# Fewer held expert tiles, shorter inverse roots and a moved scale, gate and check in a two-layer transformer kernel

## The chip, the core and the metric

The kernel runs on one core of one Trainium2 chip. The metric is the device time of one execution in microseconds (us). A core has TensorE (PE, matrix products and transposes through the PE), VectorE (DVE), ScalarE (ACT), GpSimd (POOL) and SyncE (SP); the queues of SP and POOL issue nearly all transfers here. Each engine works through its own list of instructions in order, and the engines wait for each other by semaphores.

## What is computed

Four batches of 1024 rows with 256 channels, in fp32, go through two layers. Each layer is an attention and an experts' part, and both add to x. In short:

```python
mod = (silu(c) @ wmod).reshape(4, 6, 1, 256)        # per layer: sa, ca, ga, sb, cb, gb
ga, gb = sign(ga) * max(|ga|, 0.25), sign(gb) * max(|gb|, 0.25)
x = x + ga * attention(layernorm(x) * (1 + ca) + sa)
x = x + gb * experts(layernorm(x) * (1 + cb) + sb)
```

- Layer 0's attention is causal softmax attention over 16 heads with a latent of 64. Its experts' part sends each row to the 2 of 16 experts with the largest router probability: W1, a layer norm of the hidden 256, gelu, W2, and a weighted sum of the two.
- Layer 1's attention is linear (relu, cube, normalised sums) with a convolution of three taps. Its experts' part sends each row to 1 of 8 experts, one matrix and a bias, weighted by the probability.

## The kernel before

**Stages.** `two_layers` runs four stages: the softmax attention (0 to about 510 us), `Experts0.run` (510 to 769), the linear attention (769 to about 996) and `Experts1.run` (996 to the end). x stays on chip in `k.x[b]`. The router and the sort of a batch run inside the stage before the experts that use them.

**Who sets the order.** The program is written in one order, and a planner with a cost model places each engine's instructions by that order and by when it believes the inputs to be ready. `k.pin` fixes an instruction behind the one written just before it on its engine. On top of that `Around` interleaves by hand: `tasks` are generators that yield the weight of each piece (1 or 0.5), and `k.around.step(pieces, rides)` advances the first task by that many pieces and the first of the `riders` by that many rides. Each ride issues one indirect transfer on POOL, which waits for `k.anchor`, the last big matmul written before it.

**Sorted rows.** `Sorting` (L812) counts how many rows each expert has and gives each expert whole tiles of 128 rows. `most_tiles` is the most that any routing can need: 47 tiles for each half of layer 0 (2048 rows, two experts each) and 23, 15 and 15 for the three parts of layer 1 (batches 0 and 1, batch 2, batch 3: `PARTS`). The experts run over all of them, with the expert of a tile read as an offset. `send` (L1111, L1810) fetches rows from `rows_in` and scatters them row by row into `sorted0` or `sorted1` (L928); `combine` (L1346, L1910) gathers the results back (L938) and adds them to x. The sorted buffers are cleared once with zeros on SP (L964).

**First experts.** Groups of four tiles: `arrive` (transposes, copy), `hidden` (W1, bias, statistics), `normalised` (the inverse root, then ACT), `turned` (transposes, gelu), `output` (W2, bias, store). A group's output is written two groups after its hidden part. `second_half` drains all tasks and riders before the other half's rows are loaded: at n + 2 == most, with `most` the number of groups in a half. At the start of the stage batch 3's rows (`Experts0.rows`) and the second half's sort are still tasks. The weights w2 and b2 are loaded behind the first two groups' rows.

**Inverse roots.** `rsqrt` (L72) is a bit-trick seed and three Newton steps, 13 small DVE operations. It is called for each group of the first experts and in `row_statistics` (L94), once per batch for each of the four layer norms.

**Modulation.** `setup_mod` (L166) leaves shift and scale of the attention in transposed form (`k.modT`); the experts' shift, scale and gate are stored and loaded as rows spread over the partitions (`spread_rows`, L202).

**Last experts.** `routed_rows` (L980) normalises on ACT (L992), multiplies by scale and adds shift on DVE (L1006, L1007) and stores the result in `rows_in` (L1009). `tiles_of` takes two tiles: transposes (L1870), an ACT copy (L1872), products (L1877), bias (L1883), store (L1884). `combine` weighs a gathered row on ACT (L1929), multiplies by the gate (L1937) and adds to x (L1938) on DVE in pairs, then stores the output (L1940).

**The check.** Sums that were divided by are kept, and `count_within` (L482) counts with four DVE operations over 128x512 how many lie in bounds: one count in `second_half`, two at the end of the linear attention. `out_of_bounds` (L491) adds them after the first part of the last experts; if any is out, a general version of everything runs (`tc.If(again > 0)`).

## Time and profile before

| | us |
|---|---|
| median of 3 runs (lowest, highest) | 1128.66 (1125.79, 1131.34) |
| the profiled execution | 1116.6 |
| its span, first to last instruction | 1114.8 |
| PE busy, share of the span | 966.1 (87%) |
| DVE busy | 647.1 (58%) |
| ACT busy | 612.0 (55%) |
| POOL busy | 337.5 (30%) |
| mean granted PE clock | 0.952 |
| chain that ended last | PE 63%, DVE 18%, ACT 6%, issue 5%, DMA 5% |

A timeline line gives start, length, engine, source line, operation, tiles written and read, and in brackets the idle time before it with what ended it. A matmul of fp32 counts as two instructions, so a group of four tiles has sixteen for W1 and sixteen for W2, and eight transposes. A DMA issued on SP or POOL stands as an instruction of SPq or POOL; its transfer goes on after that.

### The profile page before, as it was taken

What the parts mean: (1) busy time and instruction counts of PE and PEld (TensorE: products, weight loads), DVE (VectorE), ACT (ScalarE), POOL (GpSimd) and SP (SyncE); (2) the same over time, 40 slices, a digit from 0 to 9 for tenths busy, and PEclk for the clock granted to TensorE, in tenths of its full rate; (3) what the DMA queues carried; (4) which work ended last, traced back from release to release, by engine and by line L of the source; (5) the groups of instructions that cost most, each with busy time, mean ns of one, the idle gap of its engine ahead of it and who ended that gap; (6) DMA issues with size and microseconds to landing.
All of it is one profiled execution on the core that took longest, in us unless ns stands there. A gap on an engine that the chain in (4) does not pass through costs nothing.

```text
span 1114.8 us, 18591 instructions
## 1 busy us (share of the span) xinstructions
PE 966.1 (87%) x6158; PEld 578.1 (52%) x6158; DVE 647.1 (58%) x2143; ACT 612.0 (55%) x986; POOL 337.5 (30%) x528
## 2 busy tenths in 40 slices
PE   4999999999999998986889998887996989758761
PEld 2533434343444343335678887775564656547650
DVE  5924227313562446218767788882899969675452
ACT  0378655756476556872646765655644755423331
POOL 2022222212132156660046125301550100642732
PEclk9999999999999999998999999898998999889986
DMA  6994000000010012826446546414223201457873
GB/s 198 332 347 143 1 1 25 20 1 1 5 58 1 1 57 81 318 97 253 133 152 211 173 147 198 122 55 143 61 67 140 83 20 29 145 170 231 271 228 111
DMA packets 99016, 134.62 MB, mean 121 GB/s; under 512 B 8744, under 2 KB 86088, under 8 KB 98400
## 3 DMA queue, kind: packets, MB, share of 16 engines
q1 hardware_dynamic: 86528, 98.97, 26.6%
q0 software_dynamic: 11776, 33.57, 9.7%
q8 instruction: 53, 0.87, 0.3%
q10 hardware_dynamic: 608, 0.79, 0.2%
q14 instruction: 51, 0.42, 0.1%
HBM read 69.55 MB, written 63.75 MB: 120 GB/s over the span
## 4 chain that ended last, share of the span: by engine, by line
PE 63%; DVE 18%; ACT 6%; issue 5%; DMA 5%; POOL 1%; DVEq 0%; SPq 0%; POOLq 0%; ACTq 0%
PE ps_s L378 12%; PE ps_av L443 11%; PE ps_y L1266 6%; PE ps_qk L354 5%; PE ps_k L1456 4%; PE ps_h L1200 3%; PE ps_v L339 3%; PE ps_out L417 3%; PE ps_pr L1554 3%; DMA ys<-results,index 3%; PE ps_y L1877 2%; PE ps_q L1482 2%; PE ps_lnT L1018 1%; DVE ln_st L101 1%; ACT hid L1224 1%
## 5 line engine op out<-in xcount | busy, mean ns | idle before, releaser
L386 ACT ACTIVATE pT<-ps_s 128x1024 f32<-128x1024 f32 x288 | 279.3, 1021 | 164.3 <-PE ps_s L378 162.3
L389 POOL TENSOR_SCALAR_AFFINE_SELECT pT<-pT 128x256 f32<-128x256 f32 x256 | 105.7, 438 | 324.0 <-ACT pT L386 319.3
L378 PE MATMUL ps_s<-qT,kT 32*128 32x512 f32 (+3 forms) x1536 | 178.5, 520 | 0.5 <-ACT pT L386 0.5
L443 PE MATMUL ps_av<-pT,v 128*32 128x512 f32 (+3 forms) x1536 | 164.2, 495 | 9.7 <-DVE turned L401 6.4
L938 POOL DMA_INDIRECT ys<-results,index x96 | 101.3, 1055 | 136.7 <-DVE mv L1212 35.5
L928 POOL DMA_INDIRECT sorted<-hs,index x96 | 97.7, 1018 | 143.3 <-PE ps_y L1266 69.3
L378 PEld LDWEIGHTS ps_s<-qT,kT 32*128 32x128 f32 x1536 | 74.4, 183 | 95.5 <-issue 72.9
L1266 PE MATMUL ps_y<-w,act 128*128 x376 | 94.0, 406 | 20.5 <-ACT act L1249 20.5
L1224 ACT ACTIVATE hid<-hid,nmr,rstd 128x256 f32<-128x256 f32 x94 | 49.0, 595 | 85.2 <-DVE nmr L1220 85.1
L443 PEld LDWEIGHTS ps_av<-pT,v 128*32 128x32 f32 x1536 | 40.6, 108 | 102.6 <-issue 56.7
L1266 PEld LDWEIGHTS ps_y<-w,act 128*128 128x128 f32 x376 | 74.8, 205 | 33.8 <-ACT act L1249 23.1
L1200 PE MATMUL ps_h<-w,xT 128*128 x376 | 86.0, 380 | 1.7 <-ACT xT L1183 1.5
L401 DVE STREAM_TRANSPOSE turned<-ps_av 128x512 f32<-128x512 f32 x32 | 22.8, 713 | 97.1 <-PE ps_av L443 96.8
L1200 PEld LDWEIGHTS ps_h<-w,xT 128*128 128x128 f32 x376 | 69.4, 190 | 11.1 <-ACT xT L1183 2.4
L1877 PE MATMUL ps_y<-we,xT 128*128 x212 | 57.1, 416 | 18.5 <-ACT xT L1872 18.0
L1249 ACT ACTIVATE act<-ps_hT,gain 128x128 f32<-128x128 f32 x188 | 67.7, 461 | 4.5 <-PE ps_hT L1240 4.5
L1456 PE MATMUL ps_k<-wqkv,hT 128*128 128x512 f32 x128 | 62.4, 605 | 3.9 <-DMA wqkv<-in_wqkv_dram 3.0
L361 DVE COPY qT<-ps_qk 128x512 f32<-128x512 f32 x16 | 11.1, 691 | 79.1 <-PE ps_qk L354 79.0
L1877 PEld LDWEIGHTS ps_y<-we,xT 128*128 128x128 f32 x212 | 41.5, 207 | 27.6 <-ACT xT L1872 21.5
L1275 DVE TENSOR_TENSOR y<-ps_y,b 128x256 f32<-128x256 f32 x94 | 37.7, 419 | 24.1 <-PE ps_y L1266 23.4
L101 DVE BATCH_NORM_STATS2 ln_st<-x 128x6 f32<-128x256 f32 x128 | 49.2, 409 | 0.5
L1208 DVE TENSOR_TENSOR hid<-ps_h,b 128x256 f32<-128x256 f32 x94 | 36.5, 415 | 20.0 <-PE ps_h L1200 16.4
(218 smaller groups left out, 1526.3 us busy)
## 6 DMA issues: line engine op xcount, KB each, us to landing
xs<-sorted SPq DMA_DIRECT2D x71, 256.0 KB, 4.1
results<-y SPq DMA_DIRECT2D x71, 256.0 KB, 2.4
sorted<-zero SPq DMA_DIRECT2D x2, 6016.0 KB, 21.1
rows_in<-h SPq DMA_DIRECT2D x16, 512.0 KB, 2.9
hs<-rows_in POOLq DMA_DIRECT2D x32, 256.0 KB, 4.0
w<-in_w_dram SPq DMA_DIRECT2D x8, 1024.0 KB, 7.9
x<-in_x_dram SPq DMA_DIRECT2D x4, 1024.0 KB, 8.0
b<-in_b_dram SPq DMA_DIRECT2D x2, 2048.0 KB
```

Of the source, the lines that this page charges most:

```text
L101: nc.vector.bn_stats(st[:, t, :], k.x[b][:, t, :])
L378: k.anchor = nc.tensor.matmul(pair[hh // 2][:, hh % 2, c0 : c0 + w], lhsT=kTs[o][rows, kb * P : (kb + 1) * P], rhs=qT[rows, q1 - w : q1], ...
L386: nc.scalar.activation(pT, ps, AF.Exp, scale=1.0 / L**0.5)
L389: nc.gpsimd.affine_select(out=pT[:, :, c0 : c0 + P], in_=pT[:, :, c0 : c0 + P], compare_op=ALU.is_ge, fill=0.0, base=0, pattern=[[0, 2], [ ...
L443: nc.tensor.matmul(po[32 * hh : 32 * hh + 32, 512 - w :], lhsT=vs[b % 2][:, kb, 8 * g + 2 * hh + o, :], rhs=exps[b, g, o, u][hh // 2][:, h ...
L928: i = self.k.nc.gpsimd.indirect_dma_start(out=buffer.ap, out_offset=bass.IndirectOffsetOnAxis(ap=index, axis=0), in_=rows, in_offset=None, ...
L938: self.paced(self.k.nc.gpsimd.indirect_dma_start(out=rows, out_offset=None, in_=buffer.ap, in_offset=bass.IndirectOffsetOnAxis(ap=index, a ...
L1200: mm = nc.tensor.matmul(ph[:, j], lhsT=xTs[i // 2][:, j, cc], rhs=w1[:, cc, bass.ds(at[i + j], C)], start=cc == 0, stop=cc == CC - 1,)
L1249: o = nc.scalar.activation(act[:, j, cc], pt[:, j, cc], AF.Gelu, bias=gain[:, 1, cc, t : t + 1], scale=gain[:, 0, cc, t : t + 1],)
L1266: mm = nc.tensor.matmul(po[:, j], lhsT=acts[i // 2][:, j, cc], rhs=w2[:, cc, bass.ds(at[i + j], C)], start=cc == 0, stop=cc == CC - 1,)
L1456: k.anchor = nc.tensor.matmul(ps, lhsT=hT[:, cc, t * P : (t + 1) * P], rhs=wqkv[:, cc, C:], start=cc == 0, stop=cc == CC - 1,).ins
L1877: k.anchor = nc.tensor.matmul(po[:, j], lhsT=xT[:, j, cc], rhs=self.we[:, cc, bass.ds(at[j], C)], start=cc == 0, stop=cc == CC - 1,).ins
```

## The change

- **Fewer held tiles.** `held_tiles` holds rows // 128 + 3/4 of the experts: 44 per half, and 22, 14 and 14. One DVE operation per sort (five in all, `k.fits`) notes whether the rows fit; if not, the general version runs. The buffers keep their old size, and the part of the results that is no longer written is cleared with zeros at the same place as the sorted rows (five transfers more).
- **Shorter roots.** 10 operations: another seed, one cubic step and one Newton step.
- **Last batches.** For the parts of one batch (2 and 3) `routed_rows` no longer applies scale and shift. They are applied on ACT with per-partition operands (`k.modF`) at the two copies behind transposes: the router's `hT`, and `xT` in `tiles_of`. The gate is applied to the experts' result before its store, and `combine` becomes one DVE operation a row. The first part is unchanged.
- **Checks later.** All three counts are made in the last experts after the second part, in three row buffers (tag `xs`), and the sum and test after the third part.
- **First groups.** Three pieces of tasks are issued before the weights' loads; group 1 issues none; groups 0 and 1 no longer issue four at their end; in group 2 `turned` follows `hidden`.

The diff, cut:

```diff
-RSQRT_SEED = float(0x5F3759DF - (1 << 31))
+RSQRT_SEED = float(0x5F3759DF - (1 << 22) - (1 << 31))
+CUBIC = 1.5**0.5
...
-    nc.vector.tensor_scalar(half, var, eps, None, ALU.add)
+    nc.vector.tensor_scalar(half, var, eps, 0.5, ALU.add, ALU.mult)
...
-    nc.vector.tensor_scalar(half, half, 0.5, None, ALU.mult)
-    for step in range(3):
-        nc.vector.tensor_tensor(a, src, src, ALU.mult)
-        nc.vector.tensor_tensor(a, a, half, ALU.mult)
-        dst = out if step == 2 else y
-        nc.vector.scalar_tensor_tensor(dst, a, -1.5, src, ALU.add, ALU.mult)
-        src = y
+    nc.vector.tensor_tensor(a, src, src, ALU.mult)
+    nc.vector.scalar_tensor_tensor(a, a, CUBIC, half, ALU.mult, ALU.mult)
+    nc.vector.scalar_tensor_tensor(a, a, -5.0 / 3.0 * CUBIC, a, ALU.add, ALU.mult)
+    nc.vector.scalar_tensor_tensor(y, a, 1.25 * CUBIC * CUBIC, src, ALU.add, ALU.mult)
+    nc.vector.tensor_tensor(a, y, y, ALU.mult)
+    nc.vector.tensor_tensor(a, a, half, ALU.mult)
+    nc.vector.scalar_tensor_tensor(out, a, -1.5, y, ALU.add, ALU.mult)
...
+    for m, (shift, scale) in ((k.modT[layer], ((0, 0), (0, C))), (k.modF, ((32, C), (64, 0)))):
+        if m is k.modF and layer == 0:
+            continue
+        for i, (p, c) in enumerate((shift, scale)):
...
+            nc.vector.tensor_scalar(
+                m[:, CC * i : CC * i + CC], pt[:, :, :B], float(i), None, ALU.add
+            )
...
+def count_sums(k, pool):
+    recs = [k.recs.rearrange("p n i j -> p (n i j)")]
+    recs += [k.recs1[:, i].rearrange("p b t h -> p (b t h)") for i in range(2)]
+    inverse = 1.0 / SUM_HI, 1.0 / SUM_LO
+    for i, (rec, (low, high)) in enumerate(zip(recs, (inverse, (SUM_LO, SUM_HI), inverse))):
+        good = pool.tile([P, 8 * B * H], F32, tag="xs", name="good", bufs=6)
+        count_within(k, good, rec, low, high, k.good[:, i : i + 1])
...
+def held_tiles(k, rows, ne):
+    return most_tiles(rows, ne) if k.fits is None else rows // P + 3 * ne // 4
...
+        if k.fits:
+            nc.vector.tensor_scalar(
+                k.fits.pop(0), ends[:, 1, ne - 1 : ne], float(self.tiles), None, ALU.is_le
+            )
...
+        if scalar and scale is not None:
             nc.vector.tensor_tensor(h, h, bcast(scale, 1, 4), ALU.mult)
             nc.vector.tensor_tensor(h, h, bcast(shift, 1, 4), ALU.add)
...
-            nc.scalar.copy(hT[:, cc], ps)
+            if scale is None:
+                nc.scalar.activation(
+                    hT[:, cc], ps, AF.Identity,
+                    bias=k.modF[:, cc, b : b + 1], scale=k.modF[:, 2 + cc, b : b + 1],
+                )
+            else:
+                nc.scalar.copy(hT[:, cc], ps)
...
-            if early:
-                good = self.back.tile([P, 4, C], F32, tag="out", name="good")
-                count_within(
...
+        if early:
+            k.around.step(3)
         load_weights(w1, b1, "1")
...
-            if last:
+            if last and n > 2:
                 acts = turned(*last)
             now = hidden(hf, tiles, xTs)
-            k.around.step()
+            if last and n == 2:
+                acts = turned(*last)
+            if n != 1:
+                k.around.step()
...
-            k.around.step(2 if last else 4)
+            if last:
+                k.around.step(2)
...
-            nc.scalar.copy(xT[:, :n], ps[:, :n])
+            b = PARTS[p][0] if len(PARTS[p]) == 1 else None
+            if b is None:
+                nc.scalar.copy(xT[:, :n], ps[:, :n])
+            else:
+                for cc in range(CC):
+                    nc.scalar.activation(
+                        xT[:, :n, cc], ps[:, :n, cc], AF.Identity,
+                        bias=k.modF[:, cc, b : b + 1], scale=k.modF[:, 2 + cc, b : b + 1],
+                    )
...
+            if b is not None:
+                nc.vector.tensor_tensor(y[:, :n], y[:, :n], bcast(self.gate[:, b], 1, n), ALU.mult)
...
-                if early and p == 0:
+                if early and p + 2 == len(PARTS):
+                    count_sums(k, work)
+                if early and p + 1 == len(PARTS):
                     again = out_of_bounds(k, work, ps_x)
                 k.around.tasks.append(self.combine(p))
...
-            k.pin(nc.scalar.activation(
-                y[:, j], coming.pop(0), AF.Identity, scale=part[:, n : n + 1]
-            ))
+            if len(PARTS[p]) == 1:
+                xs = k.x[b][:, t]
+                k.pin(nc.vector.scalar_tensor_tensor(
+                    xs, ys, part[:, n : n + 1], xs, ALU.mult, ALU.add
+                ))
...
+        for buffer in k.results0:
+            buffer.clear(zero, held_tiles(k, HT * P * 2, E0))
+        for buffer, p in zip(k.results1, PARTS):
+            buffer.clear(zero, held_tiles(k, len(p) * N, E1))
```

## The prediction on record

> **What bounds the kernel now.** I read the busy slices first, then the busy time by stretch, then each engine's timeline and the waits where a stretch is not full. The slices (27.9 us each) show TensorE nearly full except at the ends of stages, and VectorE (DVE) at 8 or 9 tenths through the middle:
>
> ```profile
> PE   4999999999999998986889998887996989758761
> ...
> DVE  5924227313562446218767788882899969675452
> ```
>
> The stretches (us; its length; busy us of PE, weight loads, DVE, ACT, POOL; granted clock; DMA) are the first experts' stage in four parts, a stretch of the second attention, its end, and the last two of the last experts' stage:
>
> ```profile
> 511.00:595.00 84.00, 65.70 (x365) 54.33 (x364) 61.64 (x276) 46.57 (x100) 17.96 (x19) 0.92 0.58 199
> 595.00:631.00 36.00, 36.00 (x199) 32.12 (x198) 28.37 (x124) 21.47 (x53) 17.25 (x19) 1.00 0.61 201
> ...
> 670.00:770.00 100.00, 83.88 (x418) 71.83 (x416) 76.45 (x337) 59.39 (x146) 26.06 (x37) 0.93 0.38 115
> ...
> 820.00:870.00 50.00, 37.73 (x176) 25.43 (x174) 48.92 (x158) 25.58 (x50) 8.63 (x13) 0.90 0.33 113
> ...
> 960.00:987.00 27.00, 12.51 (x92) 9.92 (x92) 22.42 (x66) 10.29 (x18) 15.21 (x15) 0.76 0.66 212
> ...
> 1068.00:1090.00 22.00, 15.38 (x60) 12.11 (x58) 9.57 (x21) 6.34 (x13) 8.41 (x8) 0.77 0.63 203
> 1090.00:1115.00 25.00, 0.00 (x0) 0.00 (x0) 5.78 (x9) 4.06 (x8) 8.01 (x8) 0.57 0.34 104
> ```
>
> Only 595 to 670 is TensorE's alone. Before it PE idles 18.3 of 84 us, after it 16.1 of 100; 820 to 870 and 960 to 987 are DVE's; from 1090 no matmul runs. The waits of 635 to 770 (total, times, longest) say why PE idles late in the first experts: it waits for activations, and those for the inverse root:
>
> ```profile
> ACT hid L1224 <- DVE nmr L1220: 44.8, 10, 8.0
> ...
> PE ps_y L1266 <- ACT act L1249: 14.9, 6, 4.6
> ```
>
> The rows of the second half come by scatter on POOL, here first, a fetch, and last of 32, then the load that waits for them on SP, then PE at its first use (631.52, no idle noted) and at a later gap:
>
> ```profile
> 562.61 1.01 POOL L928 DMA_INDIRECT sorted<-hs,index  x1 [59.77 <-PE ps_y L1266]
> ...
> 571.05 0.76 POOL L1118 DMA_DIRECT2D hs<-rows_in  x1 [3.59 <-DMA sorted<-hs,index]
> ...
> 621.34 0.97 POOL L928 DMA_INDIRECT sorted<-hs,index  x1 [0.30 <-issue]
> ```
> ```profile
> 626.13 1.90 SPq L971 DMA_DIRECT2D xs<-sorted  x4
> ```
> ```profile
> 628.93 2.76 PE L1200 MATMUL ps_h<-w,xT 128*128 x12
> 631.52 1.04 PE L1177 MATMUL ps_xT<-ident,xs 128*128 128x128 f32 x8
> ...
> 697.90 5.12 PE L1266 MATMUL ps_y<-w,act 128*128 x16 [4.58 <-ACT act L1249]
> ```
>
> The loads were issued 3.8 us after the last scatter and take up to 4.3, so the rows land near 630.4: the scatter has about 1 us to spare. In the last stage a copy that PE needs is queued on ACT behind a gathered row:
>
> ```profile
> 1082.51 0.51 ACT L1929 ACTIVATE out<-ys,part 128x256 f32<-128x256 f32 x1 [1.25 <-DMA ys<-results,index]
> 1082.92 1.05 ACT L1872 COPY xT<-ps_xT 128x512 f32<-128x512 f32 x2
> ```
>
> **What the Trainium skill says.** "VectorE: DVE Perf Modes", section on the TRN2 errata, gives (N+151)/0.96 ns for an fp32 tensor_tensor: 161 ns at N=4, 691 at 512. The trace has 156 (L88, 128x4) and 691 (L1937): a root is bought by the number of its operations. "DMA: Bandwidth & Descriptors", section "Anatomy of one DMA", puts some 2 us of fixed cost on a transfer, most of it the receipt of the last write; here the 3.8 us above. "TensorE: Matmul & The Clock Gate", section "HAM oscillation", says that gaps above 3.4 us drop the clock; after the gap of 4.58 the sixteen matmuls took 5.12 instead of 3.62, so a long gap costs 1.5 more.
>
> **The change, part by part.** The profiled execution took 1116.6 us (span 1114.8), 1.1% under the 1128.66 median; I carry the difference in us over.
>
> *Startup and first attention.* The first root lies on the chain (L81 to L90, 15.72 to 18.15): 3 operations fewer at 0.20 apart, -0.6. Layer 1's modulation gets two more copies (0.17) and four more transposes (about 0.1) at 47 to 49: +0.4. The five added clears (9 tiles of 128 KB, 1.2 MB) go on SP behind 18.8 MB of clears; what is queued behind is the gate of batch 0, issued at 83 and first used at 168. Hidden; uncovered, 1.2 MB at 332 GB/s is 3.5. Sum **-0.2** (-1 to +3).
>
> *First experts, first half.* 47 held tiles become 44. A steady group of four takes 8.66 (602.30 to 610.96), 2.165 a tile, so three are 6.5 of PE. But the second half then starts at group 11 and needs its rows earlier, and the new order delays them. I counted the pieces: batch 3's rows and its sort have 19 or 20 left. Before, groups 0 and 1 issue 5 each and later ones 5; the sort hands over its scatters in group 3, the 32 rides (5 a group) run out in group 9, and group 10's drain finds nothing. After, 3 pieces come first, then 1, 0, 5, 5, 5: hand-over in group 4, and the drain, now in group 9, issues the last 10 scatters together, anchored to that group's hidden matmuls, whose end I call T. Early on, batch 3's normalisation goes ahead of the groups' work, but its store (L1009) then stands on SP before the fetch of group 2, which lands at 529.5 anyway (15.4 us, behind 6 MB of second weights). So T is between 595 (steady from 531) and 615 (as now); I take 605. The last scatter ends no earlier than T + 10 x 1.29 + a fetch 1.1 = 619; and no earlier than its start (565, from 560 to 572) + 32 x 1.29 + 8.4 of fetch waits = 615. Then 3.8 and 4.3: rows at 627, against 631.5 now, and PE, which wanted them at T + 8.7 = 614, has a new gap of 13 us; the clock adds 1.5. **-2.5** (-14 to +10). What is late next is the scatter.
>
> *Second half.* Three tiles, -6.5. Six gaps of y behind an inverse root (697.9 to 765.4), each root 0.6 shorter: -3.6. Dropping the count (4 DVE operations, 2.2 us) in the drain falls where DVE has room: 0. **-10.1** (-14 to -3).
>
> *Second attention.* Two roots in the full stretch 820 to 870: -1.2. At its end two counts leave DVE (0.36+0.42+0.68+0.69 and 0.43+0.43+0.68+0.66 = 4.35) and batch 2's scale and shift (4 x 1.22 = 4.9), of which the chain of waits holds 4.6 between 960 and 987; the rest hides behind the y chain (L1546). The modulated copies on ACT take 0.59 to 0.78 (L1021, L160), four of them: 0, up to +0.8. **-5.8** (-10 to -2).
>
> *Last experts.* Three tiles at 2.16 a pair are 3.2. The first part's is -1.1. The second's buys nothing: that phase (1034 to 1062) is paced by 16 gathers 1.31 apart, begun at 1038.6 and still weighted on ACT. In the third (1062 to 1090) ACT no longer holds the transposed copies behind gathers: gaps 4.5 and 1.9, with slow matmuls after them, go. DVE takes their place: three counts 6.6, seven pairs of bias and gate (0.76+0.69) 10.2, eight weighted adds (0.475, as L1371) 3.8, one bound of 20.6, against 28 now. I add 1.4 for waits: -6. The counts take three of six row buffers; the third waits for pair 18's transposes, and pair 22's load on SP for pair 19's, with results queued behind it: 0 to 2, inside that 1.4. In the tail the last gather was followed by ACT 0.51, gate 0.69, add 0.69 (with hops 2.0); now one operation 0.48: -1.5, and the last pair's gate before its store +0.7. The final test (DVE, PE, DVE, a register load on every engine) sits on POOL ahead of the last eight gathers; it ends about 1.5 us after the last y while the results need 3.3 (1090.28 to 1093.58): 0, to +1.7 if POOL's load (0.51 and 1.23 of issue at 1098) is exposed. **-8** (-13 to +2). Batch 3's missing scale and shift (4.9) shorten a sort whose rows have 20 us to spare: 0.
>
> Sum: -0.2-2.5-10.1-5.8-8 = **-26.6**, 1090.0 on the profiled execution, **1102** on the median.
>
> **Rivals.**
> *The scatter keeps up* (groups compressed fully and a sort near 555): the first half gives -13.5, in all -37.6, 1091. For it: PE's 18.3 idle us before 595. Against: the ten rides in one burst.
> *DVE gives it back*: with 40 us of DVE in the last two phases instead of 25, and a planner that places counts and weighted adds ahead of y, the last stage gives +1 and the second attention half, -2.9; -0.2-2.5-10.1-2.9+1 = -14.7, 1114.
> *Slower: the late sort.* Its pieces now compete in groups 2 to 5 with those groups' own DVE work. If its first scatter, now at 562.6, starts at S, rows come at S+59.7+8.1. The other parts give 24.1, so with 1.5 of clock it decides from S = 562.6+24.1-1.5 = 585. At the early spacing (13 us, from group 2 at 534.5), a sort ending in group 6 gives S = 590 to 594: +5 to +9, 1136. Against: half of its work stands where DVE waited.
> *Nothing gained because the fallback runs*: it would double the time. From the reference's inputs the sorts need 41, 41, 20, 12 and 13 tiles; 44, 44, 22, 14 and 14 are held. Under 1 in 100, inside the slower chance.
>
> **How the numbers follow.** A run set of this kernel can tell about 0.5% (5.6 us) from no change, 1123 to 1134.3. Forecast 0.50 (own range 1094 to 1110), scatter keeps up 0.17, DVE 0.22 (a fifth of it past 1123), late sort 0.11 (just over half of it past 1134.3). Faster: 0.50+0.17+0.18 = 0.85; same 0.04+0.05 = 0.09; slower 0.06. The range 1086 to 1122 leaves out the late sort (0.11), the DVE case past it (0.04) and what lies below 1086 (0.04).
>
> **What would show it.** PE: a gap of 9 to 17 us before the first transposes of group 11, ended by xs loads; POOL: ten scatters 1.3 apart before it. Second half 10 us shorter from there. In 960 to 987 DVE busy falls by 9. In the third phase no gap behind L1929 and DVE near full; the tail some 24 us. I am wrong if the gap before group 11 is absent, if the sort ends after group 5, or if the third phase is not shorter.

## The result, and the profile after

The kernel after takes **1117.56 us** (median of 5 runs, 1114.98 to 1119.15), the kernel before in the same set 1130.0 (1125.79 to 1131.58). The ratio is 0.9892, with an interval of 0.9866 to 0.9918: 12.4 us, where 26.6 had been forecast. Two more sets of the unchanged kernel after gave 0.9858 (0.9820 to 0.9895) and 0.9907 (0.9880 to 0.9933). The gain is about 13 us, 10 to 16 in the three sets.

The profiled execution of the kernel after took 1117.6 us (span 1115.8), its median. The one of the kernel before, from which the forecast was made, had taken 1116.6, 13 us under the 1130.0: the two profiles differ by 1 us, and the gain can't be seen between them. So I profiled the kernel before again (first experiment: 1128.3, span 1126.5) and compare with that one. The stages are cut at the first transposes of sorted rows, the first transposes of the second half, the first of the second attention, and the first of batch 3's projections behind the sort of batch 2:

| profile | start | first half | second half | second attention | last experts | span |
|---|---|---|---|---|---|---|
| before, first profile | 510.1 | 121.4 | 138.0 | 217.6 | 127.7 | 1114.8 |
| before, again | 511.5 | 120.3 | 138.7 | 221.1 | 134.9 | 1126.5 |
| after | 512.5 | 132.1 | 133.1 | 210.1 | 128.0 | 1115.8 |
| after, mean of three profiles | 512.9 | 132.8 | 130.3 | 210.8 | 127.8 | 1114.7 |
| after with the old order, mean of two | 513.1 | 116.7 | 134.1 | 210.8 | 127.9 | 1102.7 |

The old order of the last row is explained with the experiments. In the mean of the three profiles against the second row, one stage got longer, the first half of the first experts, by 12.5; the stages behind it got shorter by 25.8, and the first experts began 1.4 later. The lines that answer to those of before, busy time first, then the slices of PE and DVE (27.9 us each), where the 23rd of PE (614 to 642) shows a hole that was not there:

```profile
PE 952.5 (85%) x6072; PEld 563.6 (51%) x6072; DVE 623.2 (56%) x1987; ACT 602.6 (54%) x959; POOL 336.2 (30%) x528
...
PE   4899999999999998997789589887898798959670
...
DVE  5823236313463455216596556794689978663472
```

The stretches, with the same columns as in the prediction:

```profile
512.50:604.00 91.50, 71.60 (x393) 59.53 (x391) 64.51 (x264) 47.23 (x100) 12.74 (x14) 0.93 0.50 174
604.00:630.00 26.00, 25.47 (x137) 22.29 (x136) 18.79 (x80) 19.10 (x47) 14.86 (x16) 1.00 0.57 177
630.00:660.00 30.00, 15.38 (x80) 13.74 (x81) 11.27 (x48) 9.48 (x23) 7.83 (x9) 0.77 0.48 153
645.00:778.00 133.00, 117.21 (x594) 101.17 (x592) 94.21 (x387) 78.11 (x189) 35.88 (x45) 0.94 0.41 125
828.00:878.00 50.00, 38.42 (x177) 25.68 (x175) 48.99 (x150) 26.38 (x51) 9.11 (x13) 0.90 0.33 115
960.00:987.80 27.80, 16.16 (x120) 11.01 (x118) 18.59 (x65) 15.43 (x26) 17.91 (x19) 0.90 0.48 158
1062.00:1090.00 28.00, 20.09 (x85) 16.32 (x83) 23.07 (x50) 8.90 (x19) 10.88 (x10) 0.84 0.65 206
1092.00:1116.00 24.00, 0.00 (x0) 0.00 (x0) 4.16 (x10) 0.00 (x0) 8.00 (x8) 0.56 0.40 121
```

From 604 to 630 PE is full, and from 630 to 660 it is half idle at a clock of 0.77. The end of the second attention (960 to 987.8) still has DVE at 18.6, and in the third phase of the last experts (1062 to 1090) DVE has 23.1 of 28. The waits of the second half (645 to 778: total, times, longest):

```profile
ACT hid L1269 <- DVE nmr L1265: 27.3, 7, 6.6
...
PE ps_y L1311 <- ACT act L1294: 13.7, 7, 4.3
```

The rows' way in the kernel after: the first scatter on POOL, the first of the last eleven and the last; the loads on SP; then on PE the end of group 9's hidden part and the first use of the second half's rows:

```profile
580.50 1.22 POOL L964 DMA_INDIRECT sorted<-hs,index  x1 [75.27 <-DVE offset L950]
...
626.45 1.01 POOL L964 DMA_INDIRECT sorted<-hs,index  x1 [0.30 <-PE ps_hT L1285]
...
639.28 0.98 POOL L964 DMA_INDIRECT sorted<-hs,index  x1 [0.30 <-issue]
```

```profile
641.85 5.10 SPq L1008 DMA_DIRECT2D xs<-sorted  x6
```

```profile
617.71 3.62 PE L1245 MATMUL ps_h<-w,xT 128*128 x16
...
644.62 1.94 PE L1222 MATMUL ps_xT<-ident,xs 128*128 128x128 f32 x8 [14.63 <-DMA xs<-sorted]
```

The first scatter comes at 580.5, 17.9 later than in the first profile. From 626.45 on the last eleven stand 1.28 apart behind each other with no wait between them, and the loads are issued 2.6 after the start of the last. PE waits 14.63, and its transposes then take 1.94 instead of 1.04. In the last experts two gaps remain. The one in the second phase, behind a gathered row's weighting on ACT (the first part's), was expected to stay; the one in the third, which was to lose its gaps, is a wait for rows whose loads stood behind the counts' row buffers:

```profile
1050.31 3.76 PE L1928 MATMUL ps_y<-we,xT 128*128 x8 [4.35 <-ACT out L1992]
...
1081.57 1.94 PE L1913 MATMUL ps_xT<-ident,xs 128*128 128x128 f32 x8 [5.46 <-DMA xs<-sorted]
```

### The profile page after: what moved, and what is told of

Read it like the earlier page. It is cut to its first block, busy times and chain, and to the rows that moved or that the text cites. A ratio compares the mean times of both kernels' runs of the same rounds, so it can differ in the third digit from the quotient of the medians.

```text
span 1115.8 us, 18093 instructions
## 1 busy us (share of the span) xinstructions
PE 952.5 (85%) x6072; PEld 563.6 (51%) x6072; DVE 623.2 (56%) x1987; ACT 602.6 (54%) x959; POOL 336.2 (30%) x528
## 5 line engine op out<-in xcount | busy, mean ns | idle before, releaser
L1311 PE MATMUL ps_y<-w,act 128*128 x352 | 87.8, 405 | 16.6 <-ACT act L1294 16.0
L1311 PEld LDWEIGHTS ps_y<-w,act 128*128 128x128 f32 x352 | 69.8, 204 | 29.3 <-ACT act L1294 18.3
L1269 ACT ACTIVATE hid<-hid,nmr,rstd 128x256 f32<-128x256 f32 x88 | 45.9, 593 | 67.1 <-DVE nmr L1265 50.8
L1294 ACT ACTIVATE act<-ps_hT,gain 128x128 f32<-128x128 f32 x176 | 63.3, 458 | 15.5 <-PE ps_hT L1285 15.0
L1928 PE MATMUL ps_y<-we,xT 128*128 x200 | 54.3, 418 | 13.3 <-issue 6.0
L1320 DVE TENSOR_TENSOR y<-ps_y,b 128x256 f32<-128x256 f32 x88 | 35.2, 419 | 37.3 <-PE ps_y L1311 21.8
L1928 PEld LDWEIGHTS ps_y<-we,xT 128*128 128x128 f32 x200 | 38.7, 206 | 22.8 <-issue 8.7
L1253 DVE TENSOR_TENSOR hid<-ps_h,b 128x256 f32<-128x256 f32 x88 | 34.2, 416 | 28.6 <-PE ps_h L1245 22.5
```

What stands on the lines that cost most here:

```text
L1269: o = nc.scalar.activation(h[:, i], h[:, i], AF.Identity, bias=nmr[:, i : i + 1], scale=rstd[:, i : i + 1])
L1294: o = nc.scalar.activation(act[:, j, cc], pt[:, j, cc], AF.Gelu, bias=gain[:, 1, cc, t : t + 1], scale=gain[:, 0, cc, t : t + 1],)
L1311: mm = nc.tensor.matmul(po[:, j], lhsT=acts[i // 2][:, j, cc], rhs=w2[:, cc, bass.ds(at[i + j], C)], start=cc == 0, stop=cc == CC - 1,)
L1928: k.anchor = nc.tensor.matmul(po[:, j], lhsT=xT[:, j, cc], rhs=self.we[:, cc, bass.ds(at[j], C)], start=cc == 0, stop=cc == CC - 1,).ins
```

## The experiments

Times are medians; a ratio is always to the kernel before in the same set of runs. Where a kernel is compared in us with one of another set, the kernel before took 1130.0 to 1131.9 in both, unless it is said otherwise.

**The kernel before, unchanged.**

> The kernel before, unchanged. Its profiled execution took 1116.6 us while its runs have a median of 1128.66 to 1130.0. Theory: the profiled execution was an untypical one, so this profile shows a span near 1128, with the missing 12 us at a place that the change touches (the first use of the second half's rows, in the old profile at 631.5, now 5 to 12 later). Rival: the loss is spread over the stages, 2 to 4 us in each, by a granted clock 0.01 lower, and has nothing to do with the change. Second rival: the profile again takes 1116 to 1118 us, and profiling itself makes this kernel faster.

1130.35 against 1131.85, a ratio of 0.9979 (0.9961 to 0.9997) of one kernel to itself: so a difference of 2 us can't be relied on here, whatever its interval. The profile has a span of 1126.5. Neither the theory nor a rival describes it: of the 11.7 that it is longer than the first profile, 7.2 are in the last experts and 3.5 in the second attention, none at the rows' first use (631.78) and none by the mean clock (0.951 against 0.952). The waits of PE that nothing in the profile explains ("issue": total, times, longest) were these in the first profile,

```profile
PE ps_y L1877 <- issue: 0.3, 1, 0.3
...
PE ps_h L1200 <- issue: 0.2, 1, 0.2
```

and these in the new one:

```profile
PE ps_y L1877 <- issue: 4.4, 3, 2.1
...
PE ps_y L1266 <- issue: 2.8, 1, 2.8
...
PE ps_logits L778 <- issue: 2.3, 1, 2.3
...
PE ps_h L1200 <- issue: 0.2, 1, 0.2
```

They come to 0.5 and 9.7 us. All profiles of this study fall in two kinds. In the set where the kernel before takes 1120.4 (the runs from early_pieces to old_counts below), and in the first profile, these waits are 0.0 to 0.5 us on PE; in the sets where it takes 1130 to 1132 they are 2.5 to 17.6. What they are the profile doesn't show; the packets of the main DMA queue took the same time in both (26.6% of 1114.8 and 26.3% of 1126.5 us). The set of 1120.4 ran on one chip, the experiments' other sets on three others; one set can't show that the chip is the reason. The forecast was made on a profile of the first kind and the change measured in sets of the second.

**The order of the first groups alone**, undone in the kernel after and put into the kernel before:

```diff
-        if early:
-            k.around.step(3)
...
-            if last and n > 2:
+            if last:
                 acts = turned(*last)
             now = hidden(hf, tiles, xTs)
-            if last and n == 2:
-                acts = turned(*last)
-            if n != 1:
-                k.around.step()
+            k.around.step()
...
-            if last:
-                k.around.step(2)
+            k.around.step(2 if last else 4)
```

> The kernel after with the old order of the first groups (no three pieces ahead of the weights, a step in every group, the hidden state's transposes ahead of the next group's matmuls throughout). Theory: the new order is what delays batch 3's sort (first scatter 580.5 instead of 562.6); here the first scatter is back at 562 to 568, the gap ahead of group 11's transposes falls from 14.6 to 0 to 6, and the time falls by 8 to 12 against the kernel after, to 1106 to 1110. Rival one: the one group less before the drain makes the gap, the burst of scatters ends no earlier, and the time changes by under 3. Rival two: the new order fills early idle time of TensorE and this kernel is slower than the one after by 2 to 6.

In old_order the new order is undone: 1105.8, ratio 0.9760 (0.9728 to 0.9792), 11.8 under the kernel after, as the theory said. Its scatters are back at the old times, and PE's gap is 4.43:

```profile
564.86 1.01 POOL L964 DMA_INDIRECT sorted<-hs,index  x1 [60.43 <-DVE st L1256]
...
621.20 0.97 POOL L964 DMA_INDIRECT sorted<-hs,index  x1 [0.30 <-issue]
```

```profile
613.18 3.62 PE L1245 MATMUL ps_h<-w,xT 128*128 x16
...
629.89 1.94 PE L1222 MATMUL ps_xT<-ident,xs 128*128 128x128 f32 x8 [4.43 <-DMA xs<-sorted]
```

> The kernel before with the new order of the first groups alone (its 47 tiles, its roots, its counts). Theory: the new order delays batch 3's sort by itself: the first scatter comes at 578 to 584 instead of 564, the second half's rows some 67 later at 645 to 650 instead of 631, and the time rises by 11 to 17, to 1141 to 1147. Rival: here the drain stands one group later, so that the longer first half covers part of it, and the time rises by under 5. Second rival: the order itself gains in groups 0 to 2 and the time falls.

1148.34, ratio 1.0148 (1.0116 to 1.0180): 16.6 slower with nothing changed but the order, the theory again. The time and the first scatter lie a little beyond their ranges, and the rows' first use at 658.5 lies well beyond 645 to 650. The late first scatter, and PE's gap at the end of the half, are here too:

```profile
585.68 1.23 POOL L928 DMA_INDIRECT sorted<-hs,index  x1 [78.62 <-DVE offset L914]
...
647.10 0.97 POOL L928 DMA_INDIRECT sorted<-hs,index  x1 [0.31 <-issue]
```

```profile
658.53 1.94 PE L1177 MATMUL ps_xT<-ident,xs 128*128 128x128 f32 x8 [10.20 <-DMA xs<-sorted]
```

The pair was run once more, side by side:

> The kernel after, unchanged, beside the old order. The executions so far fall in two kinds: where the kernel before takes 1120, TensorE has under 1 us of idle time that nothing in the profile explains; where it takes 1131, it has 5 to 17. Theory: the kernel after gains about the same on both: a ratio of 0.985 to 0.990 if the kernel before is at 1131 here, 0.990 to 0.996 (1109 to 1116) if it is at 1120. Rival: the ratio is the same on both.

> The kernel after with the old order of the first groups, beside the kernel after. Theory: 10 to 15 below the kernel after whichever kind of chip this is. Rival: the new order's cost depends on the chip as the version with the early pieces did (15 to 20 below on one, 2.5 below on another): under 6 here.

1120.85 and 1105.22 (ratios 0.9907 and 0.9761, the latter 0.9726 to 0.9796): 15.6 apart, a little beyond the theory's 10 to 15. The kernel before took 1131.2 here, so the kernel after in a set of the other kind stays unmeasured.

**Which part of the order.** The same kernel with the three pieces ahead and the late transposes of group 2 kept, but the withheld pieces given back:

```diff
-            if n != 1:
-                k.around.step()
+            k.around.step()
...
-            if last:
-                k.around.step(2)
+            k.around.step(2 if last else 4)
```

> The kernel after with its three pieces ahead of the weights and its late transposes in group 2 kept, but with a step in group 1 and the four pieces at the end of groups 0 and 1 given back. Theory: withholding those pieces (1 and 0 instead of 5 and 5) is the whole delay of the sort; here its first scatter comes at 556 to 566 instead of 580.5 and the time is that of the old order or up to 3 below it, 1102 to 1107. Rival: the three pieces ahead put batch 3's normalisation on ScalarE in front of the first rows' copies, and that delays everything: first scatter 568 to 576, 1108 to 1116.

1097.95, ratio 0.9798 (0.9775 to 0.9820), in the set where the kernel before took 1120.4, beside two kernels that both have the new order, no_fold at 1112.0 and old_counts at 1115.9 (below). Its first half took 116.0, theirs 133.5 and 133.4. Their first scatters came at 581.3 and 580.6; that of this kernel:

```profile
560.24 1.01 POOL L964 DMA_INDIRECT sorted<-hs,index  x1 [55.58 <-DVE index L933]
```

So it is the withheld pieces that delay the sort, not those put ahead. How that goes is seen on PE, in batch 3's transposes (ps_lnT), in the ranks that start the sort (ps_rank), and in the last product before it hands over its scatters (ps_gain). The kernel after:

```profile
519.25 6.47 PE L1245 MATMUL ps_h<-w,xT 128*128 x16 [5.71 <-ACT xT L1228]
525.55 0.60 PE L1057 MATMUL ps_lnT<-ident,h 128*128 128x128 f32 x4
...
543.97 0.60 PE L1057 MATMUL ps_lnT<-ident,h 128*128 128x128 f32 x4
...
553.85 0.60 PE L1057 MATMUL ps_lnT<-ident,h 128*128 128x128 f32 x4
...
571.09 0.67 PE L895 MATMUL ps_rank<-some,before 128*128 128x256 f32 x2 [3.22 <-DVE some L890]
...
580.83 0.64 PE L1136 MATMUL ps_gain<-mine,g 16*128 16x44 f32 x4
```

The kernel after with the old order:

```profile
529.56 1.94 PE L1057 MATMUL ps_lnT<-ident,h 128*128 128x128 f32 x8 [7.96 <-DVE h L1046]
...
537.01 1.90 PE L1057 MATMUL ps_lnT<-ident,h 128*128 128x128 f32 x8
...
553.93 0.67 PE L895 MATMUL ps_rank<-some,before 128*128 128x256 f32 x2 [1.47 <-DVE mv L1257]
...
564.51 0.64 PE L1136 MATMUL ps_gain<-mine,g 16*128 16x44 f32 x4
```

The first transposes come 4 us earlier with the new order, but the second set of four is a piece that group 1 no longer issues; it stands behind group 2's hidden part at 543.97, and the last ones come at 553.85 instead of 537.01. The rank comes at 571.1 instead of 553.9, and the hand-over falls into group 5's hidden part instead of group 4's. The 7.96 that PE idles at 529.56 in the old order, waiting for batch 3, are cheaper than that.

**The inverse root alone**, undone in the kernel after (the 13 operations of before) and put into the kernel before:

> The kernel after with the inverse root of 13 operations again. Theory (my terms): 0.6 at the start, 3.6 in six gaps of the first experts' second half, 1.2 in the second attention: 4 to 6 slower. Rival: the gaps are set by ScalarE and the order of the pieces, the operations fall into idle time: slower by under 2. Second rival: a longer root delays the pieces of batch 3's sort too, the first scatter comes 2 to 4 later and the time rises by 7 to 10.

The 13 operations put back into the kernel after (old_roots): 1135.47, ratio 1.0026 (1.0012 to 1.0040), 17.9 slower than the kernel after, more than the theory and its rivals allowed. By the five stages of the table, against the first profile of the kernel after: +4.3, +4.9, +1.6, +4.6, +1.4. The busy time of its page:

```profile
PE 964.5 (85%) x6072; PEld 571.5 (50%) x6072; DVE 635.6 (56%) x2101; ACT 602.8 (53%) x959; POOL 337.0 (30%) x528
```

The same 6072 matmuls took 964.5 instead of 952.5, at a clock of 0.932 instead of 0.945.

> The kernel before with the shorter inverse root alone. Undoing it in the kernel after cost 17.9 us where the sum of its terms had said 5.4. Theory: a root's half microsecond makes gaps that put TensorE's clock down, which is worth as much again or more, wherever it stands: here too it gains 12 to 18, to 1113 to 1119. Rival: the 17.9 are of the kernel after alone (its sort stands on the critical path through the late scatters, and a longer root delays it): here it gains 4 to 7, to 1124 to 1127.

1119.39, ratio 0.9896 (0.9872 to 0.9919): 12.4 faster. The gain is as large as the theory said, but not by its reason: PE's busy time is 969.2 against 967.5 in before_again, so the clock gives nothing here. The stages give +0.5, -1.4, -1.6, -4.0 and -2.2, in sum -8.7 between the two profiles. DVE has 120 instructions fewer (2023 against 2143), which are 40 roots; at 0.6 each (three operations 0.20 apart, as in the prediction) that is an estimate of 24 us, of which 12 show. Why undoing the root costs 17.9 in the one kernel and bringing it gains 12.4 in the other is open.

**Fewer tiles**, two given back to each half of the first experts:

```diff
-    return most_tiles(rows, ne) if k.fits is None else rows // P + 3 * ne // 4
+    return most_tiles(rows, ne) if k.fits is None else rows // P + 3 * ne // 4 + (2 if ne == E0 else 0)
```

> The kernel after with 46 held tiles for the first experts instead of 44 (12 groups a half again instead of 11). Theory: in the first half TensorE waits for the late rows in any case, so two tiles more (4.3 us) fit into the gap of 14.6; in the second half they are paid: slower by 3 to 5, to 1120 to 1123. Rival: both halves pay and a group more brings its own waits: slower by 8 to 10. Second rival: the shorter gap keeps the clock up and the time stays within 2.

1128.51, ratio 0.9976 (0.9959 to 0.9993): 11 slower than the kernel after. That is the first rival, a little beyond its 8 to 10; the theory, that the gap hides the first half's two tiles, fails. The first half is 7.1 longer than the mean of the kernel after, and PE's gap is as long as in the kernel after (14.04): the drain comes a group later too. The last experts were 6.5 longer in this profile, though nothing was changed there, and it lies 6.7 over its own median; how the 11 divide stays open.

**Denser scatters, with the counts in a buffer of their own**, on the old order, and the buffer alone on the kernel after:

```diff
-                k.around.step(rides=1 + i // 2)
+                k.around.step(rides=2 + i // 2)
...
-        good = pool.tile([P, 8 * B * H], F32, tag="xs", name="good", bufs=6)
+        good = pool.tile([P, 8 * B * H], F32, tag="counted", name="good", bufs=1)
```

> The kernel after with the three counts in a buffer of their own instead of three of the six row buffers. Theory: the gap of 5.46 before the third part's transposes at 1081.6 (rows whose load was issued at 1077.1) goes, and the time falls by 3 to 5. Rival: VectorE is full in 1067 to 1084 and only that sets the end, so the gap becomes a wait for VectorE and the time falls by under 1.

With the buffer alone (own_counts) 1115.3, ratio 0.9847 (0.9817 to 0.9878), which can't be told from the three ratios of the kernel after, so that neither the 3 to 5 of the theory nor the rival is shown. In its profile no wait for rows over 1 us is left in the last experts, and that stage takes 125.9 instead of 127.8.

> The kernel after with the old order of the first groups, the counts in a buffer of their own, and two or three scatters a step of the outputs instead of one or two. The old order alone gave 1105.8 and the counts' buffer 2.3 less than the kernel after, 1103.5 together. Theory: the 32 scatters are then limited by the 1.3 each that they take, not by their pacing; they end at 611 to 616 instead of 621.2, the gap of 4.43 ahead of group 11 goes and the clock stays up: 1096 to 1100. Rival: the fetches between the scatters or the sort set the last one: under 2 less, 1101 to 1105. Second rival: denser scatters delay the loads and stores of the running groups: above 1105.

With both on the old order (dense_rides) 1102.88, ratio 0.9758 (0.9731 to 0.9784): the first rival, not the theory. The last scatter comes at 614.1, 7 earlier, and no wait for rows is left ahead of group 11, but the second half begins at 631.0 all the same. PE now waits elsewhere in these groups, for activations, once with a slow group after it:

```profile
601.48 5.41 PE L1311 MATMUL ps_y<-w,act 128*128 x16 [1.78 <-ACT act L1294]
...
623.07 3.72 PE L1311 MATMUL ps_y<-w,act 128*128 x16 [1.64 <-ACT act L1294]
```

> The same as early_pieces, with the counts in a buffer of their own and two or three scatters a step of the outputs instead of one or two. Theory: with an earlier sort and denser scatters the rows are there before TensorE asks for them, and the start of the second half is TensorE's own: 1097 to 1102. Rival: the rows were not late in the dense version either (1102.9), the groups' activations are what ends the waits: 1101 to 1105. Second rival: it is worse than both, over 1106, if the pieces ahead of the weights hurt.

1095.09, ratio 0.9780 (0.9756 to 0.9804), in the set of 1120.4: the lowest time of the study, 2.9 under early_pieces beside it, and PE waits for no rows in its first half. In a set of the other kind:

> The kernel after, unchanged, beside the other three of this call, since the chips differ (the kernel before took 1131.8 on one and 1120.4 on another). Theory: its ratio to the kernel before is that of its first run, 0.989, within 0.003; the stages before the last lie within 3 us of the first profile. Rival: on a chip on which the kernel before is faster it gains less, 0.993 to 0.997 (the gap of 14 us in the first experts is in absolute time).

> The kernel after with the pieces given back to groups 0 and 1, its counts in a buffer of their own and denser scatters, beside the kernel after on the same chip. Theory: the order of the pieces is worth 12 and the counts' buffer and the scatters 2 to 4 together: 13 to 17 below the kernel after, ratio to the kernel before 0.973 to 0.977. Rival: the ratio of 0.978 stays and the kernel after is at 0.993 here, 15 below in any case; only a difference under 10 would speak against the order as the cause.

1115.63 for the kernel after (0.9858) and 1113.13 for early_best (0.9826, 0.9785 to 0.9866): only 2.5 apart, where 13 to 17 had been expected. In the profile of early_best from this set the first scatter was at 562.1 and no row was late, yet the first half took 127.8 instead of 115.8, with waits for nothing that the profile shows and slow matmuls:

```profile
578.79 5.16 PE L1311 MATMUL ps_y<-w,act 128*128 x16 [2.93 <-issue]
...
610.75 1.78 PE L1311 MATMUL ps_y<-w,act 128*128 x7 [2.20 <-ACT act L1294]
...
625.14 3.72 PE L1311 MATMUL ps_y<-w,act 128*128 x16 [1.27 <-ACT act L1294]
```

By the test that I had set, a difference under 10 would speak against the order as the cause, and this one is under 10. Against that stand the old order's 11.8 and 15.6 and the 16.6 of before_new_order, all in sets of the same kind, and a pair without the fold from this very set, 1124.13 and 1112.53 (below), 11.6 apart. So the gain from giving the pieces back was 14 to 18 in the set of 1120.4, and together with the buffer and the scatters 2.5 and 11.6 here; why so little in the one pair is open. Whether the three pieces ahead of the weights help or harm isn't shown: the old order was run only in sets of the second kind.

**Scale, shift and gate of the last batches**, done as before again:

```diff
-        if len(part) > 1:
+        if True:
             scale, shift = (
...
-            b = PARTS[p][0] if len(PARTS[p]) == 1 else None
+            b = None
...
-            if len(PARTS[p]) == 1:
+            if False:
                 xs = k.x[b][:, t]
...
-            if j == 1 and len(PARTS[p]) > 1:
+            if j == 1:
```

> The kernel after with the last two batches' scale and shift ahead of the sort again and their gate at the weighted add (ScalarE's weighting with VectorE's two operations), so that neither is done at the experts' tiles. Theory (my terms): 4.9 of VectorE come back to the end of the second attention, of which 2 to 3 show, and the third phase of the last experts gets its gaps of 4.5 and 1.9 behind ScalarE back, 4 to 6: slower by 6 to 9, 1123 to 1127. Rival: VectorE is as full with the fold as ScalarE's queue was in the way without it: slower by 2 to 3, only the part at the second attention's end. Second rival: no difference or faster, since eight operations of the gate at the tiles leave VectorE.

1112.04, ratio 0.9932 (0.9907 to 0.9957), in the set of 1120.4, where the kernel after was not run. So it was repeated beside the kernel after:

> The kernel after without the fold of the last batches' scale and gate, once more beside the kernel after on the same chip. Its profile had 3.3 us more in the second attention and 4.0 less in the last experts than that of the kernel after. Theory: the fold is worth nothing: within 3 of the kernel after. Rival (my terms in the prediction): 6 to 9 slower than the kernel after.

1124.13 against 1115.63 (ratio 0.9934, 0.9915 to 0.9953, against 0.9858): 8.5 slower, as my own terms in the prediction said, here the rival. By stages against after_again: +3.9 in the second half, which the edit doesn't touch, +5.3 in the second attention, +1.9 in the last experts.

> The same without the fold of the last batches' scale and gate. Theory: with the last stage's rows no longer delayed by the counts, the fold costs as much in the last experts as it brings in the second attention: within 3 of early_best. Rival one: the fold brings its 3 in the second attention and its counterpart of 4 was the counts' collision, so that leaving it out costs 3 to 6. Rival two: leaving it out gains 3 or more.

1112.53 against 1113.13 for early_best: nothing. Its second attention is 5.3 longer than that of early_best_again, its last experts 3.1 shorter, its first half 6.5 shorter and its second half 5.6 longer, neither of which the edit touches. What both pairs agree on is the 5.3 in the second attention; in the last experts the sign differs.

**The counts at their old places:**

> The kernel after with the three counts at their old places (one at the start of the first experts' second half, two at the end of the second attention). Theory: they cost 2 to 4 at the second attention's end, where VectorE ends the waits, and give back 2 to 5 in the last experts' third phase (the gap of 5.46 before its transposes goes): within 2 of the kernel after, 1116 to 1120. Rival: at their new place they are hidden but for the row buffers, so that putting them back costs the 4.35 whole: 1120 to 1123. Second rival: they are dearer at the new place than at the old: faster by 2 to 4.

1115.94, ratio 0.9962 (0.9948 to 0.9975), in the set of 1120.4. With no kernel after beside it, this says nothing sure about theory or rivals; its second attention takes 211.8 and its last experts 127.3, both within 1.1 of the kernel after.

## Why the prediction was half wrong

The time lies in the range, and the sign was right. The size was not, by one step. Two slips in the forecast's own working change nothing: its terms for the first half give -2.9 (627.1 for 631.5, and 1.5 of clock) and not -2.5, and the slices of DVE that it calls 8 or 9 are 6 to 9 with one 2.

- **First half, forecast -2.5, measured +12.5: the failed step.** The piece count said that the sort hands over its scatters in group 4 instead of group 3, and so it did, one group later. But the forecast set their start at 565, two microseconds from where it had been, because batch 3's normalisation went ahead. The later hand-over cost some 17 instead: 580.5 to 582.6 in the three profiles, against 562.6 and 564.0 before. T, the end of group 9's hidden part, was to be 605, between 595 and 615, and is 621.3 (616.8 with the old order): dropping a group shortened the half by that group, and the idle time of its early groups was not filled. The 32 scatters were to take 49.7 with their fetches; from the start of the first to that of the last it was 58.8. The first use came 5.3 after that start, 4.4 after the last one's end, where 8.1 had been put (3.8 to the issue of the loads, measured 1.6, and 4.3). 580.5, 58.8 and 5.3 are the 644.6 of the trace.
- **Which of the two misses bound the rows.** In the forecast the drain was the binding one, T + 14 = 619, and the scatters' own start gave 615. With the measured T of 621.3 the drain would give 635 for the end of the last scatter; with the measured start of 580.5 the other term would give 630. It ended at 640.3: POOL was still busy with earlier scatters and a fetch until 626, and only then issued its last eleven. So both starting times were off by some 16, and either of them alone would have made the rows 11 to 16 us late. With 644.6 in the place of 627 the sum would have been 17.6 less, -9.0, near the measured gain.
- **A rival had the mechanism.** It was that of the slower rival, the late sort, at a price under the 585 from which it was to decide; I gave it 0.11 and drew it at 590 to 594. The sign that I had named, a gap of 9 to 17 ahead of group 11 behind a burst of scatters, came true (14.63) though the step was wrong, which is luck: PE and the rows were both some 16 late, and the difference stayed.
- **How much of the shortfall this is.** With the old order the four other parts of the change gain 26.0 (1131.24 to 1105.22; 26.05 in the other set). In the kernel after the start and the stages other than the first half gain 24.4, where my other terms had 24.1. That they agree so well is in part luck, as the next points say, and the 24.4 rest on a single profile of the kernel before.
- **Second half, -10.1 forecast, -8.4 measured** (138.7 to 130.3; single profiles 128.3 to 133.1). With the old order it is only -4.6 (134.1), so that some 3.8 of the 8.4 came with the new one, behind PE's long gap. The six gaps behind a root were to be 0.6 shorter each, 3.6 in all. That is not shown: the roots alone move this stage by 1.6 in either kernel, and PE's waits for activations were 14.9 and 18.0 in the two profiles before, 12.3 to 13.7 after, and 15.1 in old_order.
- **Second attention, -5.8 forecast, -10.3 measured.** I counted two roots in its full stretch, 1.2; the roots alone give 4.0 and 4.6 here. The fold, that is scale, shift and gate moved, gives 5.3, against my 4.6 for fold and counts together.
- **Last experts, -8 forecast, -7.1 measured against the ordinary kernel before**, but not as forecast. Against the profile that I had read it is nothing (127.7 to 127.8): that profile had almost none of the unexplained waits of this stage, 4.4 on its products in before_again. The third phase was to lose 6 by the fold; it was not the shorter one, and undoing the fold costs the whole stage 1.9 in one pair and gains it 3.1 in the other. The counts' row buffers, put at 0 to 2, made a gap of 3.7 to 5.5, but with a buffer of their own the stage is only 1.9 shorter in one profile: other waits stood behind. The tail behind the last product, 25.0 and 25.7 in the two profiles before, was to lose 0.8 and took 25.9 to 26.3. DVE in the last 27 to 28 us of the second attention fell from 22.4 to 18.6, not by 9.
- **Roots.** My terms had 9 of some 40 on the path, 5.4 in all; alone they bring 12.4. I had looked for roots where a stage was full or a gap stood directly behind one. By stages more than the forecast came in the second attention, and something in the first half and the last experts, for which it had no root at all; which roots these are is open.
- **Parts don't add.** Order +15.6, roots -12.4, fold -8.5 (0 in the other pair) and tiles -11 for two of the three in each half come to -16.3, the whole is -13, and with the old order it would be -31.9 against a measured -26.0. Each was measured in another surrounding, and where the difference goes is open.

The startup came out at +1.4 for -0.2, inside its range. Whether the fold or the new place of the counts is worth keeping in the last experts stays open.

## What to carry to other kernels

Where a chain of small pieces is issued by hand between large groups, a withheld piece can cost the length of a whole group, not its own: here the hand-over slipped by one group, and the first scatter by some 17 us. Count at which step the chain hands over, and give each step its time from the trace, before you ask which idle time the new order fills. A profile 1% under the median of its kernel is a sign to look at where it differs before its stages are used in a sum. Short dependent operations are cheap one by one; three fewer in each of 40 roots were worth 12 us here.

## What the runs showed of the hardware

- **Waits for nothing that the profile shows** differ by set: on PE 0.0 to 0.5 us in one kind, 2.5 to 17.6 in the other, with 1120.4 against 1130 to 1132 for the kernel before. Their cause is open.
- **Scatters** of 128 rows leave POOL about 1.28 apart, also eleven in a row with no wait between them; from the first to the last of the 32 of the second half it took 49 to 61 us in all kernels. From the end of the last one to the issue of the loads that wait for it, it was 1.6 in the kernel after, 2.2 and 3.8 in the two profiles before and 4.9 in old_order, so that the 3.8 of the forecast are no fixed cost.
- **The clock.** PE's busy time for the same 6072 matmuls went from 949.3 to 964.5 between kernels. The Trainium skill, "TensorE: Matmul & The Clock Gate", section "HAM oscillation", ties the lower clock to gaps above 3.4 us. The trace agrees after the gap of 14.63, where eight transposes took 1.94 instead of 1.04. But 3.4 is not the limit here: in the kernel before, the first profile, a gap of 2.82 was enough,

```profile
578.45 5.12 PE L1266 MATMUL ps_y<-w,act 128*128 x16 [2.82 <-ACT act L1249]
```

where sixteen matmuls took 5.12 instead of 3.62 at a granted clock of 0.72, while in old_order a gap of 2.72 left it at 1.00. Where the limit lies isn't shown.
